# Graph attention behind a pair stage: the first scores spread by TensorE, and the neighbours' steps placed later

## The chip, the cores and the metric

The kernel runs on one core of a Trainium2 chip. The metric is the device time of one execution in microseconds (us); lower is better. A run of a kernel is timed several times, and medians are compared.

## The reference, cut to what matters

Four graph layers follow one another, each as `x = x + layer(relu(layernorm(x)))`, on x of 8 batches, 2048 nodes and 64 features. The change lies at the end of layer 0 and the beginning of layer 1. Layer 0 ends with a choice between two feature vectors of each node:

```python
pair = jnp.stack([industry, g], axis=2)
coefs2 = jax.nn.softmax(attn_scores(pair), axis=-1)   # attn_scores(f) = tanh(f @ fcW + fcb) @ av
out = jnp.einsum('bnk,bnkf->bnf', coefs2, pair)
```

Layer 1 is attention over the neighbours of each node:

```python
h = jnp.matmul(input, W)
s_src = jnp.matmul(h, a_src)
s_dst = jnp.matmul(h, a_dst)
e = leaky_relu(s_src[:, :, None] + s_dst[:, None, :], negative_slope=0.2)
attention = softmax(where(adj > 0.5, e, -9e15), axis=2)
return elu(jnp.matmul(attention, h))
```

The exponent of a leaky relu of a sum splits into factors. With r = exp(-0.8 s_src) of the receiving node, w = exp(0.8 s_dst) and v = exp(0.2 s_dst) of the neighbour, the weight of a neighbour is proportional to v * max(r, w) * adj, and what belongs to the receiving node alone falls out in the softmax. So the kernel needs, for a pair of batches, r along the free axis and the same in all 128 partitions, and w as one column per block of 128 neighbours.

## The kernel before, in words

The activations are kept transposed: a tile holds two batches of 64 features in its 128 partitions and nodes along its free axis. There are NP = 4 such pairs p of batches; 2048 nodes are NCW = 4 chunks of CW = 512 or NT = 16 blocks of 128.

**The pair stage** is the loop at the end of `layer0`, over 16 chunks (p, c). It is spread over iterations i = 0 to 17, and in each one `first` (load of an `iv` tile through SP's queue, two products `pf`, a tanh `th_s` on ScalarE) and `second` (two more products `pf` and a tanh, a DVE operation) work on chunk i+1, `third` (product `pd` and a tanh) on chunk i-1, `differ` (a DVE subtraction) on chunk i, `fourth` (DVE) on chunk i-2. For p = 0 `fourth` makes tiles `xo` that stay in SBUF for layer 1, with two more DVE additions; for the other p it adds into memory (`xd`) through POOL's queue. `iv` has 9 buffers, so the later loads wait for writes of earlier chunks. The PSUM tiles of `pf` and `pd` have two buffers each.

**The neighbours' steps of pair 0** (`first_neighbours`) are a generator that this loop advances twice in each iteration, at its start and at its end (`next(steps, None)`), from i = 4 on. For chunks 0, 1 and then 2, 3 it goes through: `mean` on TensorE; `xc` on DVE; squares on ScalarE; `var` on TensorE; Ln and Exp on ScalarE, with two loads of its function table; the normalised `xc` on DVE; then twice the product `ph` with W1x (features and the two score columns) in one step, and its exponent `vd`, the copy `sc` and the product `hS` in the next. Ten steps for each two chunks; after twenty, one for `wd` (w) and `rs` (r, as columns), and a last one: `pr`, a transpose of `rs` on TensorE, `rr`, its copy on DVE, a DMA of `rr` to `r_dram`, and two loads `R` that read one row of `r_dram` into all 128 partitions (`scores`, once for each batch). That makes 22 steps, from the start of i = 4 to the end of i = 14. PSUM for these steps has two tags, `ln` and `h`, with one buffer each.

The order of TensorE's work is as written, once `kit.strict` is set (in `scores` of the pair stage); `V` and `A` are wrappers (`InOrder`) which do the same for DVE and ScalarE. The DMA queues and the later attention are ordered by the framework's scheduler.

**The attention** (`Layer1.run`, `attend`) goes over 4 pairs p and two halves hf of 1024 nodes. For each of 16 blocks m of neighbours DVE makes two tiles `pt` = max(R, wd) * aT (128x1024, one for each batch), TensorE multiplies them with `hS` (`o`) and sums them with `vd` (`dn`). `pt` has 6 buffers. Meanwhile the neighbours' steps of the next pair (`neighbour_steps`) are woven in, with loads `x` from memory. `attend` takes the first two R tiles from `self.first`, where `first_neighbours` put them; all others come from `scores`.

Of the kernel before, what the change touches and what calls it, by code (L numbers as in the profile page):

```python
# [8 lines left out]
FP = mybir.dt.float32  # L9
FR = mybir.dt.float32r  # L10
AF = mybir.ActivationFunctionType
# [5 lines left out]
P = 128  # L17
# [14 lines left out]
def cols(c, w=CW):  # L32
    return slice(c * w, (c + 1) * w)
# [601 lines left out]
class Kit:  # L635
# [88 lines left out]
    def mm(self, *args, **kw):  # L724

        one = self.nc.tensor.matmul(*args, **kw)  # L726
        if self.strict:
            self.tc.keep_in_program_order(one)
# [33 lines left out]
def layer0(kit, hn, x1_dram, open_early, late_tile, between):  # L762
# [6 lines left out]
    mm = nc.tensor.matmul  # L769
# [442 lines left out]
    with ExitStack() as s0:  # L1212
        io = s0.enter_context(tc.tile_pool(name="o_io", bufs=9, reuse_waits="tile"))
        sb = s0.enter_context(tc.tile_pool(name="o_sb", bufs=2, reuse_waits="tile"))
        ps = s0.enter_context(tc.tile_pool(name="o_ps", bufs=2, space=PSUM, reuse_waits="tile"))
        chunks = [(p, c) for p in range(NP) for c in range(NCW)]
        ivs, ths, tgs, ccs, xs = {}, {}, {}, {}, []

        def scores(v, f):

            act = A if kit.strict else nc.scalar
            pf = ps.tile([P, 2, CW], FP, tag="pf", name="pf")
            for b2 in range(2):
                kit.strict = kit.strict or b2 == 1
                mm(pf[:, b2, :], fcW[half(b2), :], v[half(b2), :], start=True, stop=True)
            th = sb.tile([P, 2, CW], FP, tag="th", name="th_s", bufs=5)
            act.activation(th, pf, AF.Tanh, bias=fcb, scale=f)
            return th

        def first(i):  # L1230
            p, c = chunks[i]
            iv = ivs[i] = io.tile([P, CW], FP, tag="iv", name="iv")
            nc.sync.dma_start(out=iv, in_=ind_dram[p, :, cols(c)])
            ths[i] = scores(iv, 2.0)

        def second(i):
            p, c = chunks[i]
            tgs[i] = scores(gT[p][:, cols(c)], 1.0)

            V.scalar_tensor_tensor(ivs[i], gT[p][:, cols(c)], -0.5, ivs[i], op0=OP.mult, op1=OP.add)  # L1240

        def differ(i):
            V.tensor_sub(ths[i], ths[i], tgs.pop(i))

        def third(i):
            pd = ps.tile([P, CW], FP, tag="pd", name="pd")
            th = ths.pop(i)
            for b2 in range(2):
                mm(pd[half(b2), :], Av, th[:, b2], start=True, stop=True)
            A.activation(pd, pd, AF.Tanh, scale=0.5)  # L1250
            ccs[i] = pd

        def fourth(i):
            p, c = chunks[i]
            df = ivs.pop(i)
            V.scalar_tensor_tensor(df, ccs.pop(i), 1.0, df, op0=OP.add, op1=OP.mult)
            if p:
                nc.gpsimd.dma_start(out=x1_dram[p, :, cols(c)], in_=df, accum_op=OP.add)
            else:
                V.tensor_add(df, df, gT[p][:, cols(c)])  # L1260
                V.tensor_add(xs[c], xs[c], df)
                nc.sync.dma_start(out=x1_dram[p, :, cols(c)], in_=xs[c])
            if c == NCW - 1:
                late_tile(p)

        first(0)
        kit.strict = False
        first(1)
        for c in range(NCW):
            xs.append(sb.tile([P, CW], FP, tag="x", name="xo", bufs=NCW))  # L1270
            nc.sync.dma_start(out=xs[c], in_=t["xT"][0, :, cols(c)])
        second(0)
        steps = one.first_neighbours(xs, V, A)

        for i in range(len(chunks) + 2):
            if i > 3:
                next(steps, None)
            if 0 < i < len(chunks) - 1:
                first(i + 1)
            if i < len(chunks) - 1:  # L1280
                second(i + 1)
            if 0 < i <= len(chunks):
                third(i - 1)
            if i < len(chunks):
                differ(i)
            if i > 1:
                fourth(i - 2)
            if i > 3:
                next(steps, None)
            if i in (1, 4, 8):  # L1290
                p = 1 + i // 4
                nc.gpsimd.dma_start(out=x1_dram[p], in_=gT[p], accum_op=OP.add)
        for _ in steps:
            pass
# [3 lines left out]
class Layer1:  # L1298
# [69 lines left out]
    def first_neighbours(self, xs, V, A):  # L1368


        kit, sb, ps = self.kit, self.sb, self.ps
        nc, mm = kit.nc, kit.mm
        sc = sb.tile([P, NT, 4], FP, tag="sc", name="sc", bufs=1)
        vd = sb.tile([P, NT, 2], FP, tag="vd", name="vd", bufs=1)
        wd = sb.tile([P, NT, 2], FP, tag="wd", name="wd", bufs=1)
        hS = None
        for d in (0, 2):
            q = [sb.tile([P, CW], FP, tag=g, name="q", bufs=1) for g in ("x", "q")]
            xc = [sb.tile([P, CW], FP, tag="xc", name="xc") for k in range(2)]
            mean = [ps.tile([P, CW], FP, tag=g, name="mean") for g in ("ln", "h")]  # L1380
            for k in range(2):
                mm(mean[k], kit.avg, xs[d + k], start=True, stop=True)
            yield
            for k in range(2):
                V.tensor_sub(xc[k], xs[d + k], mean[k])
            yield
            for k in range(2):
                A.activation(q[k], xc[k], AF.Square)
            yield
            var = [ps.tile([P, CW], FP, tag=g, name="var") for g in ("ln", "h")]  # L1390
            for k in range(2):
                mm(var[k], kit.avg, q[k], start=True, stop=True)
            yield
            for k in range(2):
                A.activation(q[k], var[k], AF.Ln, bias=kit.eps)
            for k in range(2):
                A.activation(q[k], q[k], AF.Exp, scale=-0.5)
            yield
            for k in range(2):
                V.scalar_tensor_tensor(xc[k], xc[k], 0.0, q[k], op0=OP.max, op1=OP.mult)  # L1400
            yield
            if hS is None:
                hS = sb.tile([P, NT, P], FP, tag="hS", name="hS", bufs=1)
            for k in range(2):
                two = []
                for g in range(2):
                    m = 4 * (d + k) + 2 * g
                    ph = ps.tile([P, 2, P + 4], FP, tag=("ln", "h")[g], name="ph")
                    for j in range(2):
                        at = (2 * g + j) * P  # L1410
                        mm(ph[:, j, :], xc[k][:, at : at + P], kit.W1x, start=True, stop=True)
                    two.append((slice(m, m + 2), ph))
                yield
                for ms, ph in two:
                    A.activation(vd[:, ms, :], ph[:, :, P : P + 2], AF.Exp, scale=0.2)
                for ms, ph in two:
                    V.tensor_copy(sc[:, ms, :], ph[:, :, P:])
                    V.tensor_tensor(
                        hS[:, ms, :].rearrange("p t (b f) -> p t b f", b=2),
                        ph[:, :, 0:P].rearrange("p t (b f) -> p t b f", b=2),  # L1420
                        vd[:, ms, :, None].to_broadcast([P, 2, 2, F]), op=OP.mult,
                    )
                yield
        A.activation(wd, sc[:, :, 0:2], AF.Exp, scale=0.8)
        rs = sb.tile([P, 2, NT], FP, tag="rs", name="rs", bufs=1)
        A.activation(rs, sc[:, :, 2:4].rearrange("p t b -> p b t"), AF.Exp, scale=-0.8)
        yield
        pr = ps.tile([2 * NT, P], FP, tag="h", name="pr")
        kit.turn(pr, rs.rearrange("p b t -> p (b t)"))
        rr = sb.tile([2 * NT, P], FP, tag="rr", name="rr", bufs=1)  # L1430
        V.tensor_copy(rr, pr)
        nc.sync.dma_start(out=self.r_dram[0].rearrange("b (t n) -> (b t) n", n=P), in_=rr)
        self.first = [self.scores(0, 0, b2) for b2 in range(2)]
        self.now = hS, vd, wd
        yield

    def scores(self, p, hf, b2):

        self.turn += 1
        r = (self.sb2 if self.turn % 3 == 0 else self.R).tile([P, HN], FP, tag="R", name="R", bufs=2 - (self.turn % 3 == 0))  # L1440
        self.kit.nc.sync.dma_start(out=r, in_=self.r_dram[p, b2 : b2 + 1, cols(hf, HN)].to_broadcast([P, HN]))
        return r

# [534 lines left out]
```

## Time and profile before

| what | us |
|---|---|
| median of 3 runs | 2093.17 (2092.11 to 2094.1) |
| profiled execution, its own time | 2096.54 |
| its span in the trace | 2094.7 |
| TensorE busy in the span | 2006.4 (96%) |
| DVE busy | 1196.8 (57%) |
| ScalarE busy | 453.1 (22%) |
| first product `pf` of the pair stage starts | 440.76 |
| last product `pd` of the pair stage starts | 521.48 |
| first `pt` of the attention starts | 534.38 |

The page has one row of digits for each engine over 40 equal slices of the span (9 is 90% busy or more) and one for the granted TensorE clock. The chain of waits follows the work that ended last backwards, from each instruction to what released it. The timeline lists instructions in order of time; "x8" are eight instructions that follow each other, and the brackets tell how long the engine was idle before and who ended that. A product of the program appears as two TensorE rows in the trace, so four products of 128 columns are eight rows. The durations of rows on one engine overlap; for the pace of an engine the starts are compared. PEld is the loading of weights, which runs beside PE.

### The profile page before, as it was taken

How to read it: one execution, taken by the hardware profiler on the slowest of the kernel's cores; microseconds unless marked ns; L12 is line 12 of the kernel's file. 1: busy time of each engine (PE TensorE's matmuls, PEld its weight loads, DVE VectorE, ACT ScalarE, POOL GpSimd, SP SyncE). 2: the span in 40 equal slices, each digit the busy share in tenths (PEclk: the TensorE clock that was granted, in tenths of full speed). 3: DMA queues.
4: the chain of work that ended last, by engine and by line, in shares of the span. 5: the costliest groups of instructions: out<-in, count | busy, mean ns of one | idle time of the engine just before them, and what ended most of it. 6: DMA issues, size and time to landing. Idle time of an engine off the chain costs nothing.

```text
span 2094.7 us, 23522 instructions
## 1 busy us (share of the span) xinstructions
PE 2006.4 (96%) x9132; PEld 1151.8 (55%) x9132; DVE 1196.8 (57%) x1882; ACT 453.1 (22%) x855; POOL 264.3 (13%) x383
## 2 busy tenths in 40 slices
PE   7999898987799999999999999999999999999997
PEld 4777655532222222226776457765477755577653
DVE  6667488966788888884223652226642256522355
ACT  4321244456111111112121111211111211112100
POOL 0211054422000000000001110002100012100022
PEclk9999899999899999999999999999999999999999
DMA  6656272156211111213110002101021001121000
GB/s 182 192 184 193 80 241 68 40 151 150 62 41 41 41 41 26 61 31 85 58 42 19 25 28 66 56 10 31 22 64 56 31 21 26 36 72 50 8 14 11
DMA packets 84538, 139.21 MB, mean 66 GB/s; under 512 B 32784, under 2 KB 33040, under 8 KB 81744
## 3 DMA queue, kind: packets, MB, share of 16 engines
q1 hardware_dynamic: 65488, 84.91, 13.5%
q0 software_dynamic: 18928, 52.70, 10.0%
q8 instruction: 74, 1.21, 0.2%
q14 instruction: 48, 0.39, 0.1%
HBM read 103.69 MB, written 37.03 MB: 67 GB/s over the span
## 4 chain that ended last, share of the span: by engine, by line
PE 57%; issue 12%; POOL 3%; DVE 2%; DMA 1%; ACT 1%; POOLq 0%; DVEq 0%; SPq 0%; ACTq 0%
PE acc L726 27%; PE o L726 11%; PE u L726 6%; PE dn L726 5%; PE py L726 2%; PE mean L726 2%; PE var L726 1%; POOL fold L1866 1%; POOL ot L1867 1%; POOL ot L1868 1%; PE ph L726 1%; DMA R<-r_dram 1%; PE prd L726 1%; PE tp L732 1%; PE pv L726 1%
## 5 line engine op out<-in xcount | busy, mean ns | idle before, releaser
L726 PE MATMUL acc<-aT,parts 128*128 128x512 f32 x1664 | 455.9, 419 | 0.0
L726 PEld LDWEIGHTS acc<-aT,parts 128*128 128x128 f32 x1664 | 307.8, 188 | 111.7 <-issue 49.4
L1473 DVE SCALAR_TENSOR_TENSOR pt<-R,wd,aT 128x1024 f32<-128x1024 f32 x192 | 236.6, 1279 | 29.5 <-DMA R<-r_dram 14.0
L726 PE MATMUL o<-pt,hS 128*64 128x512 f32 x1024 | 238.2, 602 | 13.7 <-DVE pt L1473 13.5
L1854 DVE TENSOR_TENSOR pr<-u,embf 128x512 f32<-128x512 f32 x256 | 170.7, 688 | 138.8 <-PE u L726 132.2
L726 PE MATMUL u<-W3f,y 64*128 64x512 f32 x1024 | 241.0, 589 | 0.0
L726 PEld LDWEIGHTS u<-W3f,y 64*128 64x128 f32 x1024 | 99.2, 187 | 120.6 <-issue 120.6
L726 PEld LDWEIGHTS o<-pt,hS 128*64 128x64 f32 x1024 | 68.6, 137 | 174.0 <-issue 164.9
L940 PE MATMUL acc<-at,Y 128*128 128x512 f32 x512 | 137.0, 413 | 2.9 <-DVE ev L949 2.9
L726 PE MATMUL u<-W3f,v 64*128 64x512 f32 x512 | 138.8, 619 | 0.0
L726 PE MATMUL dn<-pt,vd 128*32 128x512 f32 x1024 | 123.1, 598 | 0.0
L1690 DVE TENSOR_TENSOR yb<-py,cb_f 128x512 f32<-128x512 f32 x32 | 22.1, 691 | 173.7 <-PE py L726 173.7
L1866 POOL TENSOR_TENSOR fold<-fold 128x256 f32<-128x256 f32 x64 | 47.7, 745 | 548.4 <-DVE fold L1865 510.5
L940 PEld LDWEIGHTS acc<-at,Y 128*128 128x128 f32 x512 | 96.0, 196 | 26.0 <-issue 4.0
L726 PE MATMUL acc<-aTl,parts 128*128 128x512 f32 x384 | 103.1, 405 | 0.0
L1858 DVE TENSOR_TENSOR pr<-pr 128x512 f32<-128x512 f32 x128 | 88.1, 688 | 2.2
L1473 DVE SCALAR_TENSOR_TENSOR pt<-R,wd,aTl 128x1024 f32<-128x1024 f32 x64 | 79.8, 1282 | 11.4 <-PE dn L726 8.2
L726 PEld LDWEIGHTS acc<-aTl,parts 128*128 128x128 f32 x384 | 72.2, 188 | 21.5 <-issue 5.7
L1169 PE MATMUL pgs<-mix,S 128*128 128x512 f32 x128 | 69.7, 635 | 13.0 <-POOL mix L1168 12.4
L1168 POOL TENSOR_TENSOR mix<-ex,wt 128x512 f32<-128x512 f32 x64 | 66.6, 1042 | 76.7 <-DVE ex L1167 66.3
L1840 ACT COPY xs<-px 128x128 f32<-128x128 f32 x64 | 17.1, 268 | 272.7 <-POOL ot L1868 210.2
L1758 POOL TENSOR_TENSOR bq<-bq,xp 128x512 f32<-128x512 f32 x16 | 20.6, 1285 | 434.1 <-DVE xp L1756 395.5
(318 smaller groups left out, 2666.6 us busy)
## 6 DMA issues: line engine op xcount, KB each, us to landing
at<-in_adjT POOLq DMA_DIRECT2D x32, 512.0 KB, 4.5
raw<-in_adjT SPq DMA_DIRECT2D x64, 256.0 KB, 3.2
aT<-in_adjT POOLq DMA_DIRECT2D x12, 1024.0 KB, 5.4
xp<-xd SPq DMA_DIRECT2D x45, 256.0 KB, 3.0
R<-r_dram SPq DMA_DIRECT2D x16, 512.0 KB, 4.0
hi_dram<-hi SPq DMA_DIRECT2D x16, 264.0 KB, 2.4
lo_dram<-lo SPq DMA_DIRECT2D x16, 264.0 KB, 3.5
hhi<-hi_dram POOLq DMA_DIRECT2D x16, 264.0 KB, 3.0
```

The source lines that it names most:

```text
L726: one = self.nc.tensor.matmul(*args, **kw)
L732: one = self.nc.tensor.transpose(dst, src, self.ident)
L940: mm(acc[p], Y[h][:, m, p, :], at[:, k, :], start=m + h == 0, stop=m == NT - 1 and h == 1)
L1168: nc.gpsimd.tensor_tensor(mix, ex, wt[:, k, :, None].to_broadcast([P, B, F]), op=OP.mult)
L1169: return lambda: mm(flat(pg), S[:, k, :], flat(mix), start=k == 0, stop=k == NB - 1)
L1473: nc.vector.scalar_tensor_tensor(pt, R[b2], wd[:, m, b2 : b2 + 1], aT[m][:, s].bitcast(FP), op0=OP.max, op1=OP.mult)
L1690: nc.vector.tensor_tensor(yb, py, bias[:, None, :].to_broadcast([P, 4, P]), op=OP.add)
L1854: nc.vector.tensor_tensor(a, u[h], emb[:, i, 8 * w : 8 * w + 8, None].to_broadcast([P, 8, F]), op=OP.mult)
L1858: nc.vector.tensor_add(pr[h], pr[h], a)
L1866: nc.gpsimd.tensor_add(fold[:, :, 0:2, :], fold[:, :, 0:2, :], fold[:, :, 2:4, :])
L1867: nc.gpsimd.tensor_add(ot, fold[:, :, 0, :], fold[:, :, 1, :])
L1868: nc.gpsimd.tensor_add(ot, ot, xs)
```

## The change

Three things are edited. The loop advances the neighbours' steps from i = 5 instead of i = 4. In `first_neighbours` an empty step stands between the normalised `xc` and the first `ph`, for each two chunks. And the first two R tiles are no longer loaded from `r_dram`: for each batch two PSUM tiles `pb` of 512 columns (tags `ln` and `h`) are filled by four products each, of one column of `rs`, read as a 128x128 stationary operand, with the identity, and ScalarE copies each into half of the R tile. These are two steps of their own. `pr`, `rr` and the DMA to `r_dram` stay, behind them, since the second half of the nodes still loads its R tiles from there. With these there are 26 steps, from the start of i = 5 to the end of i = 17.

```diff
         for i in range(len(chunks) + 2):
-            if i > 3:
+            if i > 4:
                 next(steps, None)
...
             if i > 1:
                 fourth(i - 2)
-            if i > 3:
+            if i > 4:
                 next(steps, None)
...
             for k in range(2):
                 V.scalar_tensor_tensor(xc[k], xc[k], 0.0, q[k], op0=OP.max, op1=OP.mult)
             yield
+            yield
...
         A.activation(rs, sc[:, :, 2:4].rearrange("p t b -> p b t"), AF.Exp, scale=-0.8)
         yield
+
+        self.first = [self.scores(0, 0, None) for b2 in range(2)]
+        for b2, r in enumerate(self.first):
+            for k in range(2):
+                pb = ps.tile([P, 4, P], FP, tag=("ln", "h")[k], name="pb1")
+                for j in range(4):
+                    one = rs[:, b2, 4 * k + j : 4 * k + j + 1]
+                    mm(pb[:, j, :], one.to_broadcast([P, P]), kit.ident, start=True, stop=True)
+                A.activation(r[:, cols(k)], pb.rearrange("p k n -> p (k n)"), AF.Copy)
+            yield
         pr = ps.tile([2 * NT, P], FP, tag="h", name="pr")
         kit.turn(pr, rs.rearrange("p b t -> p (b t)"))
         rr = sb.tile([2 * NT, P], FP, tag="rr", name="rr", bufs=1)
         V.tensor_copy(rr, pr)
         nc.sync.dma_start(out=self.r_dram[0].rearrange("b (t n) -> (b t) n", n=P), in_=rr)
-        self.first = [self.scores(0, 0, b2) for b2 in range(2)]
         self.now = hS, vd, wd
         yield
...
         r = (self.sb2 if self.turn % 3 == 0 else self.R).tile([P, HN], FP, tag="R", name="R", bufs=2 - (self.turn % 3 == 0))
+        if b2 is None:
+            return r
         self.kit.nc.sync.dma_start(out=r, in_=self.r_dram[p, b2 : b2 + 1, cols(hf, HN)].to_broadcast([P, HN]))
         return r
```

## The prediction

> **What bounds the kernel now.** I read the 40 slices of the page first, then the chain of waits, then the windows and the timeline of the pair stage and its end (440 to 560 us). The chain is TensorE work over most of the span. In slices 9 to 11 (419 to 576 us) TensorE is less busy than at most other places:
>
> ```profile
> PE   7999898987799999999999999999999999999997
> PEclk9999899999899999999999999999999999999999
> ```
>
> The windows say where (columns: busy and instructions per engine, granted TensorE clock, share and rate of the DMA engines):
>
> ```profile
> 440.00:455.90 15.90, 14.61 (x56) 4.89 (x55) 9.01 (x12) 12.31 (x16) 2.66 (x3) 0.91 0.96 249
> 455.90:490.60 34.70, 26.32 (x90) 9.33 (x88) 21.99 (x35) 20.37 (x29) 3.71 (x5) 0.90 0.81 215
> 490.60:519.60 29.00, 23.79 (x96) 9.07 (x96) 18.86 (x32) 22.13 (x32) 5.36 (x7) 0.94 0.59 106
> 519.60:536.90 17.30, 4.10 (x10) 0.77 (x10) 5.59 (x7) 2.50 (x4) 3.42 (x4) 0.55 0.88 212
> ```
>
> In the last window TensorE works 4.1 of 17.3 us. The chain of waits of that time (start, length, what) names the cause, the trip of the scores through memory:
>
> ```profile
> 519.41 0.20 DVE rr L630
> ...
> 519.63 6.48 DMA r_dram<-rr
> ...
> 526.12 8.12 DMA R<-r_dram
> ...
> 534.38 1.29 DVE pt L1473
> ...
> 535.82 4.78 PE o L726 x8
> 540.59 1.66 PE mean L726 x2
> 542.25 1.85 PE dn L726 x16
> ```
>
> After it, TensorE is busy 163.81 of the 164 us from 536 to 700: the heads' loop is TensorE's. So what TensorE's first full step `o` gains in start time, the end of the kernel gains. Ahead of it, the timeline shows six places in which TensorE stands still for the neighbours' steps (in brackets the idle time before, and the releaser):
>
> ```profile
> 459.04 1.31 PE L726 MATMUL mean<-xo,avg_f 128*128 128x512 f32 x2 [1.98 <-DVE xo L630]
> ...
> 476.00 1.29 PE L726 MATMUL ph<-W1x,xc 128*128 128x132 f32 x8 [3.37 <-DVE xc L630]
> ...
> 483.15 1.14 PE L726 MATMUL ph<-W1x,xc 128*128 128x132 f32 x8 [1.41 <-DVE hS L630]
> ...
> 488.77 1.95 PE L726 MATMUL mean<-xo,avg_f 128*128 128x512 f32 x4 [1.55 <-DVE hS L630]
> ...
> 503.92 1.87 PE L726 MATMUL ph<-W1x,xc 128*128 128x132 f32 x8 [2.50 <-DVE xc L630]
> ...
> 511.20 1.14 PE L726 MATMUL ph<-W1x,xc 128*128 128x132 f32 x8 [1.56 <-DVE hS L630]
> ```
>
> Together 12.4 us. An iteration without them takes 2.93 us (447.15, 450.08, 453.01: TensorE is then full, four rows of `pf<-iv` in 0.97, four of `pf<-hn` in 0.97, four of `pd` in 1.0).
>
> **What the Trainium skill says.** "TensorE: Matmul & The Clock Gate", section "The HAM clock gate": TensorE drops to half its clock after an idle window of about 3.4 us and returns after a busy one. The trace agrees in size: four rows of `pf` take 1.87 us after 459.04, 476.00 and 503.92 against 0.97 otherwise, and each such spell costs 1.5 to 1.7 us. It is less clear on the condition: idle of 1.98 was enough, 1.41, 1.55 and 1.56 were not; but at 521.48, with some 1.3 us of work in the 3.4 before, `pd` ran cold (1.97 against 1.0). "ScalarE: Activation LUTs", section "What ACT_TABLE_LOAD costs": a table load is about 1283 ns (trace: 1283), and an ACTIVATE with immediate operands 186 + 0.833 N ns, 613 at 512 columns (trace: a copy of 128x512 out of PSUM takes 586). The page adds a drain of 1380 ns to a load; the trace shows none (load at 470.72, next work at 472.02).
>
> **The change, part by part.**
>
> *The order.* The built program's order shows that it does what it says: the four `pb` groups, then `pr`, stand behind the last `pd` on TensorE, their copies are the last ScalarE work before the table load, and DVE has pt, `rr`, pt.
>
> *Later start, and half a step between the normalisation and its product.* I walk the queues with the recorded durations, iteration by iteration (i; start of its first `pf`).
>
> - i=4: `mean` no longer stands ahead. The iv tile landed at 455.8 (issued 442.2, 13.6 to landing), so 455.93 (before: 460.28).
> - i=5: `mean` (1.9) fits at 458.9, xo being ready at 458.98. Then a new wait: the next iv tile lands 18.7 after 442.6, at 461.3. Start 461.4 (464.67).
> - i=6: the tile after that lands 22.3 after 443.3: 465.7 (469.64). The two waits are 0.6 and 1.3; before, they were hidden under the stalls.
> - i=7: `var` goes first (1.9), its squares just ready at 468.5, since DVE (3.9 us an iteration while it also adds xo) is behind with xc: 470.5 (477.22).
> - i=8: ScalarE's two table loads, Ln and Exp take 5.0 (470.72 to 475.75 before), now from 471.1. They stand ahead of th_s, for whose PSUM `pf` waits. The empty half step takes `ph` out of this wait, but not `pf`: 477.2 after 3.7 idle, cold (484.22). So this stall stays; what is gained is that the two `ph` follow without their own.
> - i=9 to 11: with no stalls on `ph` and `mean`: 482.8, 486.8, 491.6 (490.65, 493.58, 498.42).
> - i=12: `var` now stands at the start of an iteration and its squares behind tanh at the end of the one before; they end at 496.5, so 1.5 idle, and `var` to 498.0 (505.71).
> - i=13: 500.9 (512.27, with one `ph` more done). Its work ends at 503.9.
> - i=14: `ph` waits for the second Ln/Exp: 501.8 + 5.0 = 506.8, xc from 506.4, `ph` at 507.1 (3.2 idle, cold). By 503.92 to 509.64 of before, `pd` then ends 5.7 later, at 512.8 (518.13).
>
> So the pair stage comes 5.3 us forward, but owes one `ph` pair: its wait 1.56 and 1.07 give 515.45, the last two `pd` 517.45. The steps issue no DMA of their own here, and move past SP's and POOL's queues without waiting. The write-backs `xd` and the iv reloads behind them come earlier with the loop; the first reload needs about 6.1 + 8.5 us from 471.4 and is used at 498, so they are covered. If not, `pf` waits for the difference.
>
> *Scores by TensorE.* `rs` now waits for the last `hS`. From `pd` to the end of `rs` was 2.97 (514.19 to 517.16): 515.45 + 2.97 = 518.4, where before it was 517.16. Removed: 14.6 us of DMA (6.48 + 8.12) and two loads of 512 KB. Added on the path: four groups of four 128x128 products. No row shows them; the nearest is `ph`, 1.07 per four of 132 columns, a little less at 128 columns (1.04) and 1.79 cold. I take 1.07: 4.3 us, 518.55 to 522.85; the range is 4.2 to 7.2, and below nothing is excluded, since it is added work. Broadcast weights look free: `dn` loads such a one in 0.11. The third and fourth group wait for the copies of the first two (0.2 + 0.6 after them, while the next group of 1.07 runs): hidden. The last copy is not: 523.65. Then `pr` (0.1 + 0.28) and, ahead of the second pt on DVE, `rr` (0.2 + 0.27): pt starts at 524.45 instead of 523.8, so this order costs 0.65. Behind the waiting `pr` on TensorE stands the first `o`, which has to wait for the second pt anyway. The pt ends at 525.75, against 536.9. The first pt is free already after the second copy.
>
> The r_dram write and the load for the second half stay, off the path: that load is needed some 45 us later. ScalarE's table load (1.28) is followed by work only after `mean`: hidden.
>
> Sum: 525.75 - 536.9 = **-11.1 us**. TensorE has about 0.75 us of work in the 3.1 before that moment, so I take the first `o` and `mean` to run cold as before and nothing more to change. Span 2094.7 - 11.1 = 2083.6. The profiled execution took 2096.54, the median of the runs is 2093.17; the same difference gives **2082.0**.
>
> **The rivals.**
>
> - *The clock stays up.* The `pb` groups keep TensorE busy until 3 us before `o`. Warm, `o` takes 1.8 less and `mean` 0.7 less: -13.6, 2079.5. For it: 1.1 to 1.6 idle was harmless four times. Against: 521.48.
> - *The shift moves no time.* New waits for iv, `var` and th_s take what the old ones gave. `pd` of i=14 ends at 518.1, the owed `ph` comes on top, and everything in the tail 5.3 later: -5.8, 2087.4. For it: the Ln/Exp bursts are untouched, and each stops TensorE for 3 us and more in my own walk.
> - *Slower: the iv loop.* iv tiles 13 to 15 are loaded into buffers freed by `xd`, which stands behind two aT loads of 1 MB on POOL's queue. With a faster loop the tile may come too late. The slack is 26.6 us against 14.6 used. To decide, the trip would have to take 12 us more to be felt and some 27 more to end 4 us slower than before, 2097. DMA shares of 0.9 and a landing of 22 us speak for it; that these late loads landed in 4 to 9 us speaks against.
> - *The change doesn't do what it says*: excluded by the built order, up to a wait that the order doesn't show.
>
> **How the numbers follow.** Forecast (-8 to -13, 2080 to 2085): 0.58. Clock up, or colder spells fewer: 0.22. Shift worth little: 0.15. Slower: 0.03. No effect: 0.02. A measurement can tell about 0.2%, 4.2 us, from no change, so faster is 0.95. The range 2078.0 to 2087.0 holds the forecast with `pb` cold (+2.9), most of the warm case, and part of the third; what is left out is under 0.2.
>
> **What would show it.** Right: no DMA in the chain between `rs` and `o`; `pb` rows of about 1.05 per group from about 518.5; the second pt ending near 525.8; idle before `ph` gone three times out of four, kept once (about 3 us near 507), and a new stall of over 3 us before `pf` near 477; short waits of `pf` for iv between 460 and 466. Wrong: the last `pd` later than 520 (shift worth nothing), `pb` over 1.5 per group, `o` not following pt, or later stages that are longer than before by more than 1 us.

## The result and the profile after

| | before | after |
|---|---|---|
| median of six runs, us | 2093.64 (2090.06 to 2098.36) | 2083.04 (2080.51 to 2084.25) |
| profiled execution, its own time, us | 2096.54 | 2082.92 |
| its span, us | 2094.7 | 2081.0 |

The ratio is 0.9948 (0.9935 to 0.9962): 10.6 us less by the medians, 13.6 by the two profiled executions. Forecast were 11.1 less and 2082.0.

The page's slices of the kernel after, the rows of TensorE and of its granted clock:

```profile
PE   7999899887999999999999999999999999999997
PEclk9999899999999999999999999999999999999999
```

The dip of TensorE to 7 is still there, one slice long where it was two; the clock's 8 behind it, at 524 to 576 us before, is a 9. The windows of the kernel after, in the same stretches and columns as before:

```profile
440.00:455.90 15.90, 14.99 (x56) 5.03 (x56) 9.28 (x12) 12.58 (x16) 2.66 (x3) 0.90 0.97 252
455.90:490.60 34.70, 29.06 (x110) 10.62 (x111) 26.64 (x41) 25.29 (x35) 4.79 (x7) 0.95 0.89 232
490.60:519.60 29.00, 22.21 (x91) 8.77 (x90) 17.11 (x28) 18.50 (x30) 6.52 (x9) 0.94 0.66 130
519.60:536.90 17.30, 16.05 (x88) 6.03 (x89) 14.27 (x14) 5.52 (x8) 1.19 (x2) 1.00 0.44 91
```

TensorE now works 16.05 us of the last 17.3, not 4.1; the second window has 110 rows, not 90; the granted clock of the last one is 1.00, not 0.55. The chain of waits of the kernel after (start, length, what) has no DMA between `rs` and `o`:

```profile
518.11 0.16 ACT rs L630
518.31 3.91 PE pb L726 x32
522.24 0.60 ACT R L630
522.89 0.30 PE pr L732
523.42 1.27 DVE pt L1485
524.74 1.93 PE o L726 x6
526.67 1.05 PE mean L726 x2
527.72 1.85 PE dn L726 x16
```

Step by step it is the tail that was forecast, the four groups `pb`, the last copy, `pr`, the second `pt`, `o`, but for the first two rows of `o`: they run before the second `pt` is done (523.10 below). The timeline of TensorE shows what is left of the stalls in front of it, and the tail itself:

```profile
456.20 1.13 PE L726 MATMUL pf<-iv,fcWf 64*128 64x512 f32 x4 [0.47 <-DMA iv<-ind_dram]
461.79 1.13 PE L726 MATMUL pf<-iv,fcWf 64*128 64x512 f32 x4 [0.67 <-DMA iv<-ind_dram]
477.28 2.08 PE L726 MATMUL pf<-iv,fcWf 64*128 64x512 f32 x4 [4.16 <-ACT th_s L630]
496.24 1.98 PE L726 MATMUL var<-q,avg_f 128*128 128x512 f32 x4 [1.43 <-ACT q L630]
507.24 1.48 PE L726 MATMUL ph<-W1x,xc 128*128 128x132 f32 x8 [3.16 <-DVE xc L630]
514.38 1.14 PE L726 MATMUL ph<-W1x,xc 128*128 128x132 f32 x8 [1.41 <-DVE hS L630]
518.31 3.90 PE L726 MATMUL pb<-ident_f,rs 128*128 128x128 f32 x32 [0.80 <-ACT rs L630]
523.10 1.07 PE L726 MATMUL o<-pt,hS 128*64 128x512 f32 x2
524.74 1.93 PE L726 MATMUL o<-pt,hS 128*64 128x512 f32 x6 [0.56 <-DVE pt L1485]
527.65 1.92 PE L726 MATMUL dn<-pt,vd 128*32 128x512 f32 x16
```

The brackets are the stalls, their releasers beside them. From the end of the second `pt` (524.69; before, 536.90) to the start of `mean` it takes 2.0 us, before 3.7: TensorE's clock is up here.

How much of this is one execution's luck? The kernel before and the kernel after were each profiled a second time, timed as well:

> The kernel before once more: how much of the difference of the two profiles is the execution's. From the last ptg product to the first dn it took 102.4 us in the profile before; if the slow spells of TensorE and the waits for iv differ from one execution to the next as they do between the two profiles of the changed kernel (87.6 and 91.3), it is between 99 and 104 here. Time equal to before.

> The changed kernel once more, beside the kernel before: 10 to 14 us faster. If the profile's stage gain of 14.5 us at the first dn is what a usual execution has, the first dn is again near 527.7; if the clock at the first o differs from execution to execution, it may be near 530.

Ratios to the kernel before: 1.0002 (0.999 to 1.0014) and 0.9953 (0.9941 to 0.9966). Each ratio in this document is to executions of the kernel before that were timed beside those of the kernel in question, and what an experiment gains "by its ratio" is that share of 2093 us. But the two profiles of one kernel differ by 2 to 4 us in the pair stage. So what follows reads *where* from profiles and *how much* from timings. The trace cuts the pair stage well into three terms: from the first `pf` to the end of `rs`, on to the end of the second `pt`, on to the first `dn`; then the attention up to the first `acc` behind it. Worked out from the timelines, in us, with the waits of `pf` for `iv` beside the first:

```
                    to rs   (iv waits)  to second pt   to dn    sum    attention
before              76.4      1.0          19.7         5.3    101.4    417.1
before, again       75.8      0.0          19.2         4.2     99.2    417.3
e2 shift alone      77.0      2.2          14.2         4.5     95.6    417.3
e1 spread alone     80.1      5.8          11.1         4.4     95.6    419.9
e4 spread, gap      79.8      0.0           8.7         4.0     92.5    419.8
e3 spread, start    79.3      5.2           8.7         4.4     92.4    416.8
after               77.2      1.5           6.5         3.0     86.6    418.5
after, again        80.8      3.8           6.4         3.0     90.3    418.4
```

Mean of the two profiles of each kernel: the pair stage gives 11.9 (100.3 to 88.4), the attention takes back 1.2 (417.2 to 418.4), which leaves 10.7 beside the 10.6 of the medians. The executions of e1 and e4 that were profiled took 2097.44 and 2094.09 us, 9.7 and 5.7 more than the medians of their kernels; part of that lies ahead of the table, for their first `pf` starts at 444.8 and 445.1, those of the others at 437.3 to 441.1.

### The profile page after: what moved, and what is told of

It reads as the page before. It is cut to its first block, busy times and chain, and to the rows that moved or that the text cites. A ratio compares the mean times of both kernels' runs of the same rounds, so it can differ in the third digit from the quotient of the medians.

```text
span 2081.0 us, 23594 instructions
## 1 busy us (share of the span) xinstructions
PE 2005.6 (96%) x9164; PEld 1154.1 (55%) x9164; DVE 1196.8 (58%) x1882; ACT 455.5 (22%) x859; POOL 264.2 (13%) x383
## 4 chain that ended last, share of the span: by engine, by line
PE 68%; issue 15%; DVE 6%; POOL 4%; DMA 3%; ACT 2%; SPq 0%; POOLq 0%; DVEq 0%; ACTq 0%
PE acc L726 27%; PE o L726 11%; PE u L726 6%; PE dn L726 5%; PE acc L940 3%; PE pgs L1169 2%; PE var L726 2%; PE mean L726 2%; PE py L726 2%; POOL fold L1878 1%; DVE ex L1167 1%; DMA at<-in_adjT 1%; PE ph L726 1%; POOL ot L1879 1%; DMA iv<-ind_dram 1%
```

## The experiments

**The spread alone (e1).** The kernel after with the old start and without the empty step.

```diff
-            if i > 4:
+            if i > 3:
...
             yield
-            yield
             if hS is None:
```

> Spread by TensorE as in the change, but the neighbours' steps start at i=4 and have no empty step, as before. Theory (the spread carries most of the gain, the later steps the rest): the pair stage stays as before, rs ends near 517.2, the pb groups run at 518.1 to 522.0, in front of the last two pd; the last tanh and DVE step then end near 525.9 and the second pt near 528.4, against 536.9 before and 524.7 with the whole change. First dn near 531 if TensorE's clock stays up, 533.7 if not: 8.5 to 11 us faster than before, 3.5 to 6 us slower than the change. Rival (the shift moves no time): as fast as the change within 1 us. Rival (the shift carries it): within 3 us of before.

Median 2087.73, ratio 0.9973 (0.9963 to 0.9984): 5.6 us less than before by its ratio, half of the change. Lines of its chain of waits from `rs` on:

```profile
524.62 0.24 ACT rs L630
524.87 2.01 ACT th_s L630 x2
...
527.93 2.05 PE pb L726 x16
529.98 1.01 PE pd L726 x4
530.99 0.22 PE pr L732
531.21 1.03 PE pd L726 x4
532.26 0.59 ACT pd L630
...
533.48 1.29 DVE pt L1484
...
534.82 4.59 PE o L726 x8
```

The last iterations of the pair stage now stand among the spread: two tanh of 2.01 behind `rs`, two `pd`, and DVE's last work before `pt`. From the end of `rs` to the first `pt` it takes 8.62. The tail is as reckoned (11.1 us from `rs` to the end of the second `pt`, 11.2 expected). The size was missed: in this profile `iv` waits of 5.8 put `rs` later and the attention takes 2.7 more than before, and by its ratio too the gain is 5.6 and not 8.5 to 11.

**The shift alone (e2).** The kernel before with the later start and the empty step, R still from memory.

```diff
-            if i > 3:
+            if i > 4:
...
             yield
+            yield
             if hS is None:
```

> The later start and the empty steps as in the change, but the first R tiles are loaded from memory as before. Theory: the last pd ends near 517.5 and not 523.5, but rs ends near 518.3 and not 517.2, so the trip through memory starts no earlier; with the same landings (6.5 and 8.1 us) the first pt starts at 533 to 534.5 and the time is that of before within 1.5 us. If the landings shrink to what they are elsewhere (1.7 and 4.0), up to 8 us faster. Rival (the shift carries the gain by itself): 5 us faster or more with landings as before.

Median 2090.28, ratio 0.9995 (0.9985 to 1.0006): 1.0 us less by its ratio, 3 at most, not told from nothing. Its chain:

```profile
515.68 0.28 DVE rr L630
...
515.98 4.09 DMA r_dram<-rr
...
520.09 6.16 DMA R<-r_dram
...
526.38 1.29 DVE pt L1474
```

The last `pd` ends at 514.5 here, well before R is there, and TensorE waits for R. From the first `pf` to the start of the trip it takes 77.7 us (438.3 to 516.0), before 78.9 and 78.2: the shift brings the pair stage forward and not the scores, whose steps begin an iteration later. So little is left of it in the time. (In this one profile the trip itself was short, 10.25 against 14.6 and 13.4 in the two of before, so its stage looks better than its timing.)

**Each half of the shift, with the spread (e3, e4).** e3 is the kernel after without the empty step; e4 has the empty step and the old start.

```diff
# e3
             yield
-            yield
             if hS is None:
# e4
-            if i > 4:
+            if i > 3:
```

> The change without the empty step ahead of ph: spread and later start alone. Theory: the stall on xo at 459 is gone, those of ph on xc (over 3 us) and of ph and mean on hS (1.4 to 1.6 each) are back, and the first pf of i=14 starts near 513 instead of 508.6, but with one ph pair less to do; pb near 518 to 522, in front of the last pd; second pt near 527, first dn near 530 (clock up) to 532.4: 2 to 5 us slower than the change. Rival (the empty step moves no time): same as the change within 0.5 us.

> The change with the start at i=4 as before: spread and the empty step alone. Theory: the stall of mean on xo at 459 (2 us and a spell of slow clock) is back, the later ones on hS are gone; pb stands in front of the last pd; second pt near 527, first dn near 530 to 532.5: 2 to 5 us slower than the change. Rival (the start moves no time, since iv tiles land only at 461 and 466 anyway): same as the change within 0.5 us.

e3: 2083.71, ratio 0.9953 (0.9937 to 0.9970), the change's own. e4: 2088.38, 0.9974 (0.9964 to 0.9985), that of e1. Both had been expected 2 to 5 us slower than the change; that came true of e4 alone. So with the spread the later start is worth some 5 us, and the empty step nothing that a timing shows. What the empty step does, TensorE's list of waits of e3 tells (sum, times, longest):

```profile
PE ph L726 <- DVE xc L630: 5.9, 2, 3.4
PE pf L726 <- DMA iv<-ind_dram: 5.2, 2, 2.6
PE ph L726 <- DVE hS L630: 3.1, 2, 1.6
PE o L726 <- DVE pt L1484: 2.4, 1, 2.4
PE mean L726 <- DVE hS L630: 1.6, 1, 1.6
```

`ph`, `mean` and `var` (0.5) wait 11.1 us for neighbours' steps. The kernel after waits 10.7: 4.16 of `pf` for th_s, 3.16 and 1.41 of `ph`, 0.50 and 1.43 of `var`. The empty step exchanges stalls for others. In e4 the stall of the old start is back, and so is a long stall before `ph`:

```profile
463.79 1.86 PE L726 MATMUL mean<-xo,avg_f 128*128 128x512 f32 x2 [1.98 <-DVE xo L630]
...
513.17 1.17 PE L726 MATMUL ph<-W1x,xc 128*128 128x132 f32 x8 [3.16 <-DVE xc L630]
```

But the profiles do not show where the 5 us of the later start come from. Behind `rs` e3 and e4 both take 8.7 to the second `pt`, and their pair stages are equally long (92.4 and 92.5), with 5.2 us of waits for `iv` in e3 and none in e4; the 3.0 by which e4 is longer stand in the attention (419.8 against 416.8), far behind the edit.

**The clock at the first `o` (e5, e5b).** The kernel before, with products that nobody reads behind the pair stage, so that TensorE is busy while R is on its way.

```diff
+        one.keep_busy(xs)
...
+    def keep_busy(self, xs):
+        idle = self.ps.tile([P, CW], FP, tag="ln", name="idle")
+        for k in range(11):
+            self.kit.mm(idle, self.kit.avg, xs[0], start=True, stop=True)
```

> The kernel before, with 22 products of avg and xo (128x512) behind the last pd on TensorE, into a PSUM tile that nobody reads: they keep TensorE busy for about 10.4 us while the scores go through memory. Theory (the start of the attention is cold before, and warm in the change's profile): o and mean run warm behind the second pt, first dn near 539.8 instead of 542.2, the time 2.3 us shorter than before. Rival (the speed of the first o has nothing to do with TensorE's idle time): first dn at 542 or later, the time as before.

e5 had 22 such products, and I had forgotten that each is two rows: 44 rows took 20.19 us, longer than the gap, so `o` waited for them, and the time was 2097.03, ratio 1.0017 (1.0004 to 1.003). It says only that `o` and `mean` behind such rows take 2.93. e5b has half of them:

> The kernel before, with 11 products of avg and xo behind the last pd on TensorE (22 rows of 0.46 us, 10.1 us in all, since each product is two rows), into a PSUM tile that nobody reads; they end some 2 us ahead of the second pt. Theory (o and mean run at the slow clock before because TensorE stood idle): from the second pt to the first dn it takes 2.9 us and not 5.3, so the time is 2.3 us shorter than before, at the edge of what a timing tells. Rival: the pace of the first o as before.

TensorE's timeline of e5b:

```profile
523.72 10.53 PE L726 MATMUL idle<-xo,avg_f 128*128 128x512 f32 x22
535.00 3.10 PE L726 MATMUL o<-pt,hS 128*64 128x512 f32 x8 [0.75 <-DVE pt L1479]
538.02 1.12 PE L726 MATMUL mean<-x,avg_f 128*128 128x512 f32 x2
539.08 1.92 PE L726 MATMUL dn<-pt,vd 128*32 128x512 f32 x16
```

Eight rows of `o` take 3.10 and not 4.78, though they still start on the first `pt` alone. From the second `pt`'s end to `dn` it is 3.0 us, as in the kernel after, against 5.3 and 4.2 in the profiles before. Median 2090.77, ratio 0.9988 (0.9977 to 0.9998), 2.5 less by its ratio: the clock at this place is worth 1.2 to 2.3 by the profiles, and the timing agrees as far as it can tell (0.4 to 4.8 less).

**`rr` off DVE (e6).** In the kernel after, `rr` stands ahead of the second `pt` on DVE; here ScalarE copies it.

```diff
-        V.tensor_copy(rr, pr)
+        A.activation(rr, pr, AF.Copy)
```

> The change with rr copied from PSUM by ScalarE instead of DVE, so that nothing stands between the two pt on DVE. Theory (the copy rr, which waits for pr, delays the second pt): the second pt starts at the end of the last copy of R, near 522.9 instead of 523.4, first dn near 527.1 instead of 527.65: 0.5 us faster, less than a timing tells. Rival (pr on TensorE in front of o is what holds it): first dn unchanged.

Median 2084.89, ratio 0.9952 (0.9933 to 0.9971). From the start of `pb` to the first `dn` it is 8.82 us, against 9.34 and 9.35 in the two profiles of the kernel after. The cost of that order is there, 0.5 us, below what a timing tells.

**No Ln (e7).** To price the stalls that are left. The normalisation's Ln is left out, and with it both loads of the function table for each two chunks; the kernel then computes another normalisation.

```diff
-                A.activation(q[k], var[k], AF.Ln, bias=kit.eps)
-            for k in range(2):
-                A.activation(q[k], q[k], AF.Exp, scale=-0.5)
+                A.activation(q[k], var[k], AF.Exp, scale=-0.5)
```

> The change with the logarithm of first_neighbours left out, so that the normalisation of pair 0 is computed from exp(-var/2): ScalarE loads no function table there and works 1.2 instead of 5.0 us for each two chunks. Theory (what is left of the stalls, 4.16 us before pf at 477 and 3.16 before ph at 507, is the wait for ScalarE's Ln and Exp): both shrink to under 1 us, no slow clock after them, first dn near 519 instead of 527.65: 7 to 10 us faster. Rival (iv landings, DVE or the write-backs come next and hold it): 0 to 4 us.

Median 2072.82, ratio 0.9892 (0.9875 to 0.9909): some 10 us below the kernel after. Its list of TensorE's waits in the pair stage begins:

```profile
PE pf L726 <- DMA iv<-ind_dram: 9.3, 4, 2.9
PE var L726 <- ACT q L630: 1.9, 2, 1.4
PE ph L726 <- DVE hS L630: 1.6, 1, 1.6
```

The waits of `pf` for th_s (4.16) and of `ph` for xc (3.16) are gone: it was Ln, Exp and their tables that held both up. The waits for `iv` are no consequence of that: all four stand between 440 and 459, ahead of the first Ln. Why they are longer here than in the kernel after (1.5 and 3.8) stays open. An exponent of -0.5 on another engine, which would keep the result, wasn't tried on the chip.

**Late additions (e8, e9).** The loads of `iv` at the start of the stage share the DMA engines with three additions of 1 MB from `gT`. In e8 POOL issues these behind a copy of one column of `xo`, at 458 to 466 instead of 442 to 445; e9 is e8 and e6 together.

```diff
+        G = InOrder(tc, nc.gpsimd)
+        seen = sb.tile([P, 1], FP, tag="seen", name="seen", bufs=1)
...
-            if i in (1, 4, 8):
-                p = 1 + i // 4
-                nc.gpsimd.dma_start(out=x1_dram[p], in_=gT[p], accum_op=OP.add)
+            if i in (2, 3, 4):
+                p = i - 1
+                G.tensor_copy(seen, xs[i - 2][:, 0:1])
+                G.dma_start(out=x1_dram[p], in_=gT[p], accum_op=OP.add)
```

> The change, with the three writes of gT into xd (1 MB each) issued by POOL only after a copy of one column of xo of chunk 0, 1 and 2, that is near 455, 459 and 463 us and not near 442. Theory (the iv loads of the pair stage land late because these writes share the DMA engines with them): the iv tiles land within 10 us, the waits of pf for iv (1.5 us in the first profile of the change, 3.8 in the second) fall under 1 us, and the time is 1 to 3 us shorter than the change's. Rival (the iv loads are late for other traffic, or what follows waits for DVE's xc anyway): waits gone but first dn at the same distance from ptg, or the later iv loads come late instead.

> The change with both the late writes of gT and rr copied by ScalarE. Theory: 1.5 to 3.5 us shorter than the change, ratio to before near 0.994; rival: no different from the change.

The landing of the `iv` loads issued from 434 to 447, of the kernel after:

```profile
DMA to landing us min/median/max: 5.6/13.6/21.0
```

and of e8:

```profile
DMA to landing us min/median/max: 5.8/6.4/6.6
```

So those writes are what delays `iv` (in e9 too the latest lands after 6.7); in e8 no `pf` waits for it. Yet a timing shows no gain over the change: 2085.17, 0.9946 (0.9927 to 0.9964), and 2084.97, 0.9961 (0.9944 to 0.9977) for e9. `var` waits 2.7 now, not 1.9: 0.8 us of a wait that was covered comes out. The profile of e8 also starts the stage in a spell of slow clock (eight rows of `pf` in 3.78, in the kernel after 2.96), and both have another in the attention (below). So what the gone waits are worth isn't shown. No version that does all the work beat the change.

## Why the prediction was right, point by point

- **Size and sign.** -11.1 forecast, -10.6 by the medians; the sum is made of parts that came close, and of two that were missed and nearly cancel. By the means of the table the time to the second `pt` fell by 10.1 where 11.1 was forecast; the way on to `dn` fell by 1.8 and the attention grew by 1.2, where nothing was forecast for either.
- **The walk through the queues.** Starts of the first `pf`, forecast and measured: i=4 455.93 and 456.20; i=7 470.5 and 470.12; i=8 477.2 and 477.28, with the new stall of 3.7 (4.16); i=11 491.6 and 491.82; i=13 500.9 and 501.08; `ph` at 507.1 and 507.24; the last `ph` at 514.4 and 514.38. The waits for `var` came where they were put (0.50 and 1.43). Those for `iv` came in part: 0.67 at i=5 as forecast, none of the 1.3 at i=6, and 0.47 at i=4 that was not. Of four stalls before `ph` the walk had left two, and two were left, 3.16 and 1.41; "gone three times out of four", in the list of signs, doesn't follow from the walk and was not seen. The agreement owes something to luck: the waits for `iv` were 1.5 us in this profile and 3.8 in the next, where i=8 starts 40.1 us behind the first `pf`, and not 36.2.
- **The later start and the half step.** Their joint price on top of the spread was 11.1 less the 5.8 of the second rival, 5.3; e1 against the change gives 5.0. But it isn't two parts: the empty step gave nothing that a timing shows (e3), and I would have said that waits of `ph` gone are a gain. I had walked both edits only together.
- **The trip through memory.** 14.6 us of DMA are gone, and `pb` took 3.9 us for four groups, 0.98 each, against 1.07 taken and 1.04 as the lower value. That and shorter gaps at the copy and `pr` brought the second `pt` to 523.42, not 524.45.
- **What failed: "so I take the first `o` and `mean` to run cold as before".** They ran warm, in both profiles of the kernel after and in those of e6 to e9, and that was the price of the first rival, 1.2 to 2.3 us of its 2.5. e5b shows the same gain without any of the change's parts. The step that failed is that `o` waits for the second `pt`: its first product needs the first `pt` alone and ran at 523.10, 1.07 us long, so that behind `pb`, which ran until 522.2, TensorE stood idle for 0.69 and 0.56 only. In e1, e3 and e4, where one idle of 2.4 to 2.6 stands before `o`, it did run cold.
- **"Nothing more to change" later: failed by 1.2 us.** At the change from pair 2 to pair 3 the attention stands still a little longer. The chain of waits of the kernel after there:

```profile
832.02 6.73 DMA R<-r_dram
...
838.85 1.30 DVE pt L1485
...
840.19 1.93 PE o L726 x6
```

and of the kernel before:

```profile
845.78 4.93 DMA R<-r_dram
...
850.84 1.16 DVE pt L1473
...
852.04 1.30 DVE pt L1473
...
853.38 1.93 PE o L726 x6
```

The third of three R loads lands in 6.7 us in place of 5.6, `o` waits 1.03 and then 1.43 for `pt` where before it waited once, 1.17. Both profiles of the kernel after, e1, e4 and e6 to e9 have the longer landing (6.5 to 6.8), e3 has not (5.4), though R comes from TensorE there too. Those loads and the two `xp` loads beside them are the same in all these kernels. Why they land later stays open. Behind these two waits the six rows of `o` take 1.93 in the kernel after and in e7, but 3.3 to 3.6 in e1, e4, e6, e8 and e9: a spell of slow clock, and the rest of what makes the attention of e1 and e4 longer.

- **The rivals.** "The shift moves no time" holds, as far as timings tell, for the shift alone (e2) and the empty step, and is false of both edits together beside the spread: `rs` comes no sooner in any kernel of the table than in the two profiles of before (first column: 76.4 and 75.8, all others above), but the shift puts the last `pd` and tanh ahead of it, and what is left behind `rs` shrinks from 11.1 to 6.5. Either edit alone brings 8.7 there, though, and the timings of e3 and e4 differ; this tail is a part of the account, not all of it. The slower rival's place was quiet: no `pf` waits for `iv` after 470.

## What to carry to other kernels

Two edits that each shorten one of two chains that end together are priced together or not at all: the shift was worth 1 us alone, not told from nothing, and 5 behind the spread. Ask of a step moved later not when the loop ends, but what still stands behind the last value that the next stage needs. And before counting a removed stall as gain, look which wait is covered by it: here two of `ph` and one of `mean` went and one of `pf` and one of `var` came, and `iv` loads that landed sooner bared a wait for `var`.

## What the runs showed of the hardware

- TensorE's clock fell at shorter idles than the Trainium skill has it ("TensorE: Matmul & The Clock Gate", section "The HAM clock gate", an idle window of about 3.4 us): one idle of 2.4 to 2.6 us before `o` was enough for eight rows in 4.1 to 4.6 us (e1, e3, e4), while 0.69 and 0.56 (kernel after), or 0.75 (e5b), left it up; and at 521.48 in the kernel before two idles of 1.15 and 0.84 us went ahead of four rows of `pd` in 1.97, elsewhere 1.08. But the length of an idle doesn't decide alone. Behind 3.16 us before `ph` e4 ran on at full pace (eight rows in 1.17, four of `pf` in 1.13), and e8 took 2.13 for the same eight; behind the waits of 1.0 to 1.2 and 1.3 to 1.5 us in the attention six rows of `o` took 1.93 in some profiles and 3.3 to 3.6 in others. What else decides, no run here shows.
- A product whose stationary operand is one column read 128 times is no slower than `ph`: 0.98 us for eight rows of 128 columns, 0.122 a row, beside 1.07 for eight of 132. With a copy of 0.6 us of ScalarE for each 512 columns that spreads a vector of 1024 for two batches in 4.5 us from the first `pb` to the last half of R, in place of 10.3 (e2) to 14.6 (before) through memory.
- Loads of 256 KB landed up to 21 us after issue with three 1 MB additions on another queue, and in 6.7 at most where those came later (e8, e9).
- The same kernel's pair stage differs by 2 to 4 us between executions, in the waits for `iv` (1.0 and 0.0 before, 1.5 and 3.8 after) and in spells of slow clock (the second profile of before starts the stage in one, with eight rows of `pf` in 3.79, the first in 2.97, and then no `pf` waits for `iv`); a single profile can't weigh an edit of that size.
